# Loading the first two chunks of a weight matrix in pieces, in a LoRA and expert kernel on one core

## Chip, cores and metric

The kernel runs on one core of a Trainium2 chip. The metric is the device time of one execution in microseconds; the profile is one further execution recorded by the hardware profiler. TensorE is the matrix engine (PE in the profile, PEld its weight loads), VectorE is DVE, ScalarE is ACT, GpSimd is POOL, and SyncE (SP) only issues DMAs here. A queue named SPq or ACTq is the instruction stream of that engine where it issues DMAs.

## What is computed

All tensors are float32. x has shape (8, 512, 2048): 8 batches of 512 tokens.

```python
# conditioning layer: a dense layer and a LoRA adapter picked per batch
cond = einsum('bti,oi->bto', x, W) + b                    # W 2048 x 2048
A, Bm = lora_As[itok], lora_Bs[itok]                      # one of 32 slots, rank 16
cond = cond + 2 * einsum('btr,bro->bto', einsum('bti,bir->btr', x, A), Bm)
# top-1 routed low-rank layer, 8 experts of rank 16
logits = einsum('bsd,ed->bse', cond, route_w)
v, idx = top_k(logits, 1)
weight = one_hot(idx) * v
h  = einsum('bsd,erd->bser', cond, A_ffn)
out = x + einsum('bser,eor->bso', weight * h, Bw_ffn)
```

## The kernel before

The conditioning layer feeds only linear maps of 136 columns (8 experts x rank 16, and 8 routing columns), so the kernel never forms it. It multiplies W by the projection first. The tensor `proj` (2048 x 136) lies in `pj` as 16 blocks of 128 rows, and the kernel builds c = W^T x proj, adds each batch's adapter product, and gets a matrix m of 2048 x 136 per batch. Then each of 32 token tiles (128 tokens) takes 16 matmuls with m (`heads`, L452), a routing on VectorE (`route`) and the expert output (`delta`, L546), added to x and stored.

The change lies in the first stage. W comes in 16 chunks of 128 rows and 2048 columns, 1 MB each; chunk `oc` is loaded by `load_w(oc)` (L101) into one of four buffers. A row of a chunk is 8 KB of contiguous memory. For each chunk, `chunk_w(oc)` regroups the columns into 16 blocks `j` of 128, the order in which the tokens' transposes will need them: block j takes, from each quarter i of the row, 32 columns at 32 j. The copy (L274) writes two halves, `wv0` with j 0 to 7 and `wv1` with j 8 to 15, each in two buffers. ScalarE copies the first half and VectorE the second; for chunk 0 each half is copied by both engines, a quarter of the chunk per copy. When the copy is issued, the load of chunk `oc + 4` follows on SyncE, and for chunks 0 and 1 four more blocks of `pj` ahead of it. `fold_w(oc)` (L285) then does 16 matmuls, one for each j, with the block of `wv` as weights and `pj[:, oc, :]` as data; each float32 matmul shows as two instructions. The 16 results stay in PSUM over all chunks.

Every engine's order is written out by hand (`manual_schedule`), and each engine runs its instructions in program order. DMAs from SyncE and ScalarE also take turns on eight completion semaphores, so that a DMA is held until the transfer eight places earlier has landed.

The first loads stand on SyncE as chunk 0, chunk 1, `pj` blocks 3 to 4, chunk 2, `pj` 5 to 7, chunk 3. ScalarE issues `pj` block 0, blocks 1 to 2 and `it_i` (the adapter numbers, sent to all 128 partitions, 32 bytes each). Meanwhile TensorE runs passes over a tile of constants, `pm` (L132), whose result nobody reads:

```python
for _ in range(14):
    nc.tensor.matmul(pm, warm, warm, start=True, stop=True)
```

Between the chunks of the main loop stand other pieces of work: the adapters' row numbers (L160 to L166) and gathers (L167, L179) after chunks 4 and 7, transposes of the adapter (L316) from chunk 8 on, and the first tokens' moves.

Of the kernel before, what the change touches and what calls it, by code (L numbers as in the profile page):

```python
# [18 lines left out]
def kernel(  # L19
# [30 lines left out]
    nc = tc.nc  # L50
    P = 128
    Q = 32
    NQ = P // Q
# [6 lines left out]
    NJ = D // P  # L60
# [7 lines left out]
    HJ = NJ // 2  # L68
# [25 lines left out]
    def load_pj(c0, c1, eng=nc.sync):  # L94
        eng.dma_start(out=pj[:, c0:c1, :], in_=proj_v[:, c0:c1, :])  # L95

    w_tiles = []

    def load_w(oc):
        wt = wpool.tile([P, D], F32, tag="w", bufs=4, name=f"w_{oc}")  # L100
        nc.sync.dma_start(out=wt, in_=w[ts(oc, P), :])  # L101
        w_tiles.append(wt)

    load_pj(0, 1, nc.scalar)
    load_w(0)
    load_w(1)
    load_pj(3, 5)
    load_w(2)
    load_pj(5, 8)
    load_w(3)  # L110

    x_tiles = {}

# [14 lines left out]
    load_pj(1, 3, nc.scalar)  # L128
    nc.scalar.dma_start(out=it_i, in_=itok.to_broadcast([P, B]))
    pm = ps_s.tile([P, P], F32, tag="s", name="pm")  # L130
    for _ in range(14):
        nc.tensor.matmul(pm, warm, warm, start=True, stop=True)  # L132

    own_i = const.tile([P, B], I32, name="own_i")
# [123 lines left out]
    wv_tiles = {}  # L258

    def chunk_w(oc):  # L260
        copies = (nc.scalar.copy, nc.vector.tensor_copy)
        wv = [
            wpool.tile([P, HJ, P], F32, tag=f"wv{h}", bufs=2, name=f"wv{h}_{oc}")
            for h in range(2)
        ]
        wr = w_tiles[oc].rearrange("p (i j a) -> p j i a", i=NQ, a=Q)
        for h in range(2):
            wv_tiles[oc, h] = wv[h]
            dst = wv[h].rearrange("p j (i a) -> p j i a", a=Q)

            n = HJ // 2 if oc == 0 else HJ
            for k in range(HJ // n):
                copy = copies[1 - k] if oc == 0 else copies[h]
                copy(dst[:, ts(k, n)], wr[:, ds(h * HJ + k * n, n)])  # L274
        if oc + 4 < NO:
            if oc in (0, 1):
                load_pj(8 + 4 * oc, 12 + 4 * oc)
            load_w(oc + 4)
# [95 lines left out]
    def first_products(some, copy=nc.vector.tensor_copy):  # L374
# [4 lines left out]
        for z in some:  # L379
            m, _ = place(0, z)  # L380
            copy(m, banks[z][:, : pieces[z][2], :])

    chunk_w(0)
    for oc in range(NO):
        if oc + 1 < NO:
            chunk_w(oc + 1)
# [207 lines left out]
    for n in range(2 * NT + 4):  # L594
        t, h = divmod(n, 2)
# [36 lines left out]
        u, k = divmod(tq, TPU)  # L632
# [50 lines left out]
```

## Time and profile before

| what | value |
|---|---|
| median of 3 runs | 326.45 us (325.96 to 326.55) |
| the profiled execution | 326.17 us |
| its span in the profile | 324.4 us |
| L285, all matmuls of the folding stage | 512 instructions, 61.7 us busy, mean 280 ns |
| L132, passes over constants | 28 instructions, 6.2 us busy, mean 419 ns |
| L274, regrouping copies of half a chunk | ScalarE 1.05 us, VectorE 0.69 us |
| DMA issues of W | 16 of 1024 KB, median 11.4 us from issue to landing |

A line of the timeline gives the start and the length in microseconds, the engine, the line, the operation, what it writes and reads, how many instructions were merged, and in brackets the idle time of the engine before it with what ended it. Instructions of TensorE overlap, so their mean length is more than the distance between their starts. In the DMA windows, q1 is SyncE's queue and q10 ScalarE's; a percentage is the time of its packets as a share of the 16 DMA engines in that window. A packet is one contiguous run of memory.

### The profile page before, as it was taken

The numbers are of one execution on the slowest core, as the hardware profiler recorded it, in microseconds if no ns is written. First come the engines' busy times: TensorE is split into PE (matmuls) and PEld (weight loads), VectorE is DVE, ScalarE is ACT, GpSimd is POOL, SyncE is SP. The second block draws the span as 40 slices with busy tenths as digits, with TensorE's granted clock in tenths as the row PEclk, the third lists the DMA queues.
The fourth block names the chain that finished last, engine by engine and source line by source line (L and its number), as shares of the span: only waits on it lengthen the run. The fifth ranks groups of instructions, "written<-read, shape, count | busy, mean of one in ns | idle before, by whom it ended". The sixth has DMA issues, their size and how long they took to land.

```text
span 324.4 us, 5611 instructions
## 1 busy us (share of the span) xinstructions
PE 318.7 (98%) x2168; PEld 252.6 (78%) x2168; DVE 230.1 (71%) x408; ACT 185.4 (57%) x230; POOL 164.9 (51%) x180
## 2 busy tenths in 40 slices
PE   8999999999999999999999999999999999999994
PEld 8999999999776777777768677767676777766762
DVE  2123183468879788887887888788787887888864
ACT  3223247527958567748764976596567758770000
POOL 1002149998967676257717771946295357710000
PEclk9999999999999999999999999999999999999999
DMA  7999999953933385859395949585876759334437
GB/s 281 365 404 421 420 418 420 421 231 120 401 129 129 131 284 235 301 233 368 153 375 229 361 165 395 184 353 165 355 255 266 270 250 358 162 162 179 174 144 250
DMA packets 15306, 88.52 MB, mean 273 GB/s; under 512 B 1696, under 2 KB 4016, under 8 KB 4912
## 3 DMA queue, kind: packets, MB, share of 16 engines
q1 hardware_dynamic: 14112, 85.45, 67.2%
q0 software_dynamic: 320, 2.11, 1.6%
q10 hardware_dynamic: 848, 0.61, 0.6%
q8 instruction: 17, 0.28, 0.4%
q14 instruction: 9, 0.07, 0.1%
HBM read 54.60 MB, written 33.55 MB: 272 GB/s over the span
## 4 chain that ended last, share of the span: by engine, by line
PE 94%; DMA 4%; SPq 0%; ACT 0%; DVE 0%; issue 0%; DVEq 0%; ACTq 0%
PE ph L452 37%; PE po L546 32%; PE pc L285 16%; PE pa L361 4%; DMA w<-in_w_dram 4%; PE pg L330 1%; PE pw L508 1%; PE pe_o L546 1%; PE pbT L316 1%; PE pe_h L546 1%; ACT wv L274 0%; DVE x L559 0%; PE pq L339 0%; PE pe_s L546 0%; SPq L101 0%; SPq L95 0%
## 5 line engine op out<-in xcount | busy, mean ns | idle before, releaser
L242 POOL COPY xq<-x 32x1024 f32<-32x1024 f32 x121 | 126.7, 1047 | 77.4 <-DMA x<-in_x_dram 26.7
L242 ACT COPY xq<-x 32x1024 f32<-32x1024 f32 x135 | 140.9, 1044 | 12.0 <-DMA x<-in_x_dram 10.0
L452 PEld LDWEIGHTS ph<-m,xT 128*128 128x128 f32 x1024 | 124.7, 190 | 20.6 <-issue 16.1
L452 PE MATMUL ph<-m,xT 128*128 128x136 f32 x1024 | 129.5, 280 | 0.0
L546 PE MATMUL po<-fb,whT 128*128 128x512 f32 x240 | 111.6, 592 | 0.0
L559 DVE TENSOR_TENSOR x<-x,po 128x1024 f32<-128x1024 f32 x60 | 72.9, 1216 | 30.6 <-PE po L546 30.4
L220 DVE STREAM_TRANSPOSE xT<-xq 128x1024 f32<-128x1024 f32 x64 | 78.9, 1236 | 2.4 <-ACT xq L242 2.4
L546 PEld LDWEIGHTS po<-fb,whT 128*128 128x128 f32 x240 | 41.7, 190 | 32.0 <-issue 32.0
L285 PE MATMUL pc<-pj,wv 128*128 128x136 f32 x512 | 61.7, 280 | 0.2 <-ACT wv L274 0.2
L285 PEld LDWEIGHTS pc<-pj,wv 128*128 128x128 f32 x512 | 60.1, 190 | 1.1 <-ACT wv L274 0.4
L513 ACT COPY whT<-pw 128x128 f32<-128x128 f32 x32 | 8.5, 267 | 54.8 <-PE pw L508 54.5
L274 DVE COPY wv<-w 128x1024 f32<-128x1024 f32 (+1 forms) x17 | 12.7, 754 | 30.8 <-PE pc L285 17.8
L274 ACT COPY wv<-w 128x1024 f32<-128x1024 f32 (+1 forms) x17 | 16.9, 998 | 28.5 <-DMA w<-in_w_dram 21.8
L504 POOL TENSOR_TENSOR m<-m,c 128x408 f32<-128x408 f32 (+1 forms) x28 | 24.5, 905 | 1.3 <-ACT m L499 0.8
L499 ACT COPY m<-pa 128x408 f32<-128x408 f32 (+1 forms) x28 | 10.4, 456 | 17.6 <-PE pa L361 17.6
L167 POOL DMA_INDIRECT raw<-in_cond_b_dram,brow_i x1 | 1.4, 1434 | 24.4 <-DVE brow_i L166 24.4
L361 PE MATMUL pa<-g,ad_q 32*128 32x136 f32 x256 | 12.7, 288 | 0.0
L361 PEld LDWEIGHTS pa<-g,ad_q 32*128 32x128 f32 x256 | 10.6, 184 | 1.3
L207 POOL COPY ad_q<-raw 32x384 f32<-32x384 f32 x12 | 6.4, 536 | 9.3 <-DMA raw<-in_cond_a_dram,arow_i 8.9
L508 PEld LDWEIGHTS pw<-ident,wh 128*128 128x128 f32 x32 | 4.5, 141 | 7.4 <-issue 7.2
L463 DVE TENSOR_TENSOR ph<-ph,c0b 128x136 f32<-128x136 f32 x32 | 9.1, 284 | 1.5 <-PE ph L452 1.5
L473 DVE TENSOR_TENSOR wh<-ph,rw 128x128 f32<-128x128 f32 x32 | 9.3, 291 | 1.1
(65 smaller groups left out, 119.7 us busy)
## 6 DMA issues: line engine op xcount, KB each, us to landing
x<-in_x_dram SPq DMA_DIRECT2D x32, 1024.0 KB, 9.3
out_dram<-x SPq DMA_DIRECT2D x30, 1024.0 KB, 4.9
w<-in_w_dram SPq DMA_DIRECT2D x16, 1024.0 KB, 11.4
out_dram<-x SPq DMA_DIRECT2D x6, 256.0 KB, 2.7
fb<-in_ffn_b_dram SPq DMA_DIRECT2D x1, 1024.0 KB, 13.7
pj<-in_proj_dram SPq DMA_DIRECT2D x2, 272.0 KB, 10.8
out_dram<-x ACTq DMA_DIRECT2D x1, 256.0 KB, 2.4
pj<-in_proj_dram SPq DMA_DIRECT2D x1, 204.0 KB, 11.3
```

The lines of the kernel that those rows point to most:

```text
L220: nc.vector.transpose(dst[:, ts(h, HJ), :].rearrange("p j (g t) -> p g j t", t=Q), src.rearrange("p g (j a) -> p g j a", a=Q)[:, :, ts(h, ...
L242: copy(xq_tiles[u][ts(i, Q), :, g, :], x_tiles[u][ts(g, Q), :, ts(i, DQ)])
L274: copy(dst[:, ts(k, n)], wr[:, ds(h * HJ + k * n, n)])
L285: nc.tensor.matmul(pc[:, k, :], wv_tiles[oc, h][:, j, :], pj[:, oc, :], start=(oc == 0 and k == 0), stop=(oc == NO - 1), skip_group_check= ...
L361: nc.tensor.matmul(banks[z][:, n, :], ad_q[ts(q, Q), b // 2, 3 * part + n, :], g4[ts(q, Q), b, :], start=True, stop=True, tile_position=(q ...
L452: nc.tensor.matmul(ph_tiles[t][:, :NP], xT_tiles[t][:, j, :], m[j // JC][:, j % JC, :], start=(j == 0), stop=(j == NJ - 1),)
L463: nc.vector.tensor_tensor(ph, ph, c0b, ALU.add)
L473: nc.vector.tensor_tensor(wh.rearrange("p (e r) -> p e r", r=R), ph[:, :ER].rearrange("p (e r) -> p e r", r=R), rw.unsqueeze(2).to_broadca ...
L499: nc.scalar.copy(m, pa)
L504: nc.gpsimd.tensor_tensor(m, m, c, ALU.add)
L546: nc.tensor.matmul(part, whT_tiles[t], fb[:, ds(c, n)], start=True, stop=True)
L559: nc.vector.tensor_tensor(xs, xs, part, ALU.add)
```

## The change

Chunk 0 is loaded in four transfers of 256 KB and chunk 1 in two of 512 KB. Each transfer holds four (or eight) blocks j, which are a run of 128 (or 256) columns in each quarter of the row. VectorE does all four regrouping copies of chunk 0, each for one transfer. For chunks 1 and 2 the engines trade halves: VectorE the first, ScalarE the second; from chunk 3 on it is as before. Chunks 2 and 3 are each issued ahead of the `pj` blocks that stood in front of them. The passes over constants go from 14 to 8.

```diff
+    PIECES = {0: 4, 1: 2}
     def load_w(oc):
         wt = wpool.tile([P, D], F32, tag="w", bufs=4, name=f"w_{oc}")
-        nc.sync.dma_start(out=wt, in_=w[ts(oc, P), :])
+        n = NJ // PIECES.get(oc, 1)
+        for k in range(NJ // n):
+            dst, src = (
+                m.rearrange("p (i c) -> p i c", i=NQ)[:, :, ds(k * n * Q, n * Q)]
+                for m in (wt, w[ts(oc, P), :])
+            )
+            nc.sync.dma_start(out=dst, in_=src)
         w_tiles.append(wt)

     load_pj(0, 1, nc.scalar)
     load_w(0)
     load_w(1)
+    load_w(2)
     load_pj(3, 5)
-    load_w(2)
+    load_w(3)
     load_pj(5, 8)
-    load_w(3)
...
-    for _ in range(14):
+    for _ in range(8):
         nc.tensor.matmul(pm, warm, warm, start=True, stop=True)
...
     def chunk_w(oc):
-        copies = (nc.scalar.copy, nc.vector.tensor_copy)
+        copies = [nc.scalar.copy, nc.vector.tensor_copy]
+        if oc < 3:
+            copies.reverse()
...
-            n = HJ // 2 if oc == 0 else HJ
+            n = min(NJ // PIECES.get(oc, 2), HJ)
             for k in range(HJ // n):
-                copy = copies[1 - k] if oc == 0 else copies[h]
+                copy = copies[h] if oc else nc.vector.tensor_copy
                 copy(dst[:, ts(k, n)], wr[:, ds(h * HJ + k * n, n)])
```

## The prediction

> **What bounds the kernel now.** I read the table of busy time first, then TensorE's waits, then the start in order of time, then the DMA traffic in short windows.
>
> ```profile
> PE 318.7 (98%) x2168; PEld 252.6 (78%) x2168; DVE 230.1 (71%) x408; ACT 185.4 (57%) x230; POOL 164.9 (51%) x180
> ```
>
> TensorE is busy for 98% of the span. Its waits over the whole run are two:
>
> ```profile
> PE pm L132 <- DVE warm_a L87: 1.1, 1, 1.1
> PE pc L285 <- ACT wv L274: 0.2, 1, 0.2
> ```
>
> So from 14.87 us on, where the second wait ends, TensorE has no gap that the profile counts. Whatever moves that moment moves the end by the same amount, unless a later wait takes over. The timeline shows what stands before it:
>
> ```profile
> 1.06 6.16 PE L132 MATMUL pm<-warm 128*128 128x128 f32 x28 [1.06 <-DVE warm_a L87]
> 1.68 0.49 ACTq L129 DMA_DIRECT2D it_i<-in_itok_dram  x1
> 6.00 1.14 ACT L274 COPY wv<-w 128x512 f32<-128x512 f32 x2 [3.33 <-DMA w<-in_w_dram]
> 7.06 7.58 PE L285 MATMUL pc<-pj,wv 128*128 128x136 f32 x64
> 8.76 1.05 ACT L274 COPY wv<-w 128x1024 f32<-128x1024 f32 x1 [1.61 <-DMA w<-in_w_dram]
> 13.77 1.05 ACT L274 COPY wv<-w 128x1024 f32<-128x1024 f32 x1 [3.97 <-DMA w<-in_w_dram]
> 14.87 26.21 PE L285 MATMUL pc<-pj,wv 128*128 128x136 f32 x224 [0.23 <-ACT wv L274]
> 16.98 1.05 ACT L274 COPY wv<-w 128x1024 f32<-128x1024 f32 x1 [2.16 <-DMA w<-in_w_dram]
> 24.02 1.05 ACT L274 COPY wv<-w 128x1024 f32<-128x1024 f32 x1 [2.25 <-DMA w<-in_w_dram]
> 26.51 0.69 DVE L274 COPY wv<-w 128x1024 f32<-128x1024 f32 x1 [0.90 <-DMA w<-in_w_dram]
> ```
>
> The copies that end a wait on the DMA give the landings: chunk 0 at 6.00, chunk 1 at 8.76, chunk 2 at 13.77, chunk 3 at 16.98, chunk 5 at 24.02, chunk 6 at 26.51. TensorE folds a chunk in 3.74 us (26.21 / 7), so two chunks from 7.06 are done at 14.64; chunk 2 is ready at 13.77 + 1.05 = 14.82, and starts at 14.87. **The start of chunk 2 is the gate**, and it is a DMA gate: chunk 2 comes 5.01 us after chunk 1, where a chunk alone takes 2.49 (24.02 to 26.51). The DMA windows say why (8:9, 9:10, 14.4:16.4 and 26:28 us, in this order):
>
> ```profile
> DMA packets 463, 0.23 MB, mean 231 GB/s; under 512 B 129, under 2 KB 457, under 8 KB 457
> q1 hardware_dynamic: 234, 0.16, 62.3%
> q10 hardware_dynamic: 229, 0.07, 26.4%
> ...
> DMA packets 102, 0.28 MB, mean 276 GB/s; under 512 B 47, under 2 KB 70, under 8 KB 70
> ...
> DMA packets 546, 0.75 MB, mean 374 GB/s; under 512 B 29, under 2 KB 486, under 8 KB 486
> ...
> DMA packets 116, 0.83 MB, mean 414 GB/s; under 512 B 15, under 2 KB 15, under 8 KB 15
> ```
>
> Rows of 8 KB move at 414 GB/s. Rows of 544 B (pj) move slower, and at 9 to 10 us, while it_i's 128 rows of 32 B pass, the rate is 276 GB/s with the engines busy 79% of the time. Of the 2.52 us beyond a lone chunk, pj's 24 rows per engine (all of c3-4, half of c1-2) are 24 x 0.028 = 0.67; about 1.85 us are left for it_i.
>
> **The change, part by part.** Times are counted at chunk 2's start.
>
> 1. *Passes 14 to 8.* The 28 instructions start 0.214 us apart ((7.06 - 1.06) / 28); 16 of them end at 1.06 + 3.43 = 4.5 us. This frees TensorE 2.5 us earlier. It is worth nothing at chunk 2's start if the data isn't earlier.
>
> 2. *Chunk 0 in four pieces, chunk 1 in two.* Bytes stay; rows shrink from 8 KB to 512 B and 1 KB, since a piece takes four separate runs of each row. That is 2048 + 1024 packets for 256, or per engine 128 + 64 for 16. Price of a packet: 8 KB takes 2.49 / 8 = 0.311 us, 26.3 B/ns. In window 8:9 the two queues show 88.7% of 16 engine-us for 463 packets, six of them 8 KB: (14.2 - 1.9) / 457 = 27 ns for at most 544 B. Between landings, chunk 2 to 3 takes 3.21 - 2.49 = 0.72 us for pj's 24 rows per engine: 30 ns. The payload of 544 B at 26.3 B/ns is 20.7, so 6 to 9 ns are fixed. Packets overlap (shares over 100% elsewhere), so the lower end may be 4. With 6.5 ns: chunk 0 is 128 x (19.5 + 6.5) = 3.33 against 2.49, +0.84; chunk 1 is 64 x (38.9 + 6.5) = 2.91, +0.42. **Sum +1.25 us**; at 4 ns +0.8, at 9 ns +1.75.
>  A rule says otherwise: the Trainium skill, "DMA: Bandwidth & Descriptors", Specifications, gives 512 B as the smallest transfer at line rate. By it the sum is 0. The trace's 27 to 30 ns for 544 B is 30 to 45% over line rate, so I take the trace, and keep 0 as the far end.
>
> 3. *pj c3-4 moves behind chunk 2.* Sixteen rows per engine leave the path: 16 x 0.028 = **-0.45**. They are due at chunk 3, behind 0.58 us of slack (16.98 + 1.05 against 14.87 + 3.74), and chunk 3 now also has pj c5-7 (24 rows, 0.67) behind it instead of ahead: covered.
>
> 4. *Chunk 2's first half on VectorE.* 0.69 instead of 1.05 from landing to TensorE: **-0.36**. The second half on ScalarE is due 1.87 us later. VectorE's four copies of chunk 0 (4 x 0.425 = 1.7) and 0.69 of chunk 1 stand one after another, each under the arrival of the next piece (256 KB, 0.83 us): no cost. If pieces came together, the last would wait 1.3 us, still far ahead of its matmuls.
>
> 5. *it_i, pj c1-2 on ScalarE's queue.* Unmoved in program, but now met by SP's short rows. The two queues alternate packet by packet: in window 8:9 they moved 234 and 229. ScalarE's 32 rows per engine therefore pass beside the first 32 to 64 of SP's, not after chunk 1. it_i's 1.85 us falls upon pieces 0 to 1, and still ahead of chunk 2: the sum to chunk 2 doesn't change. 0 here, ends -1.5 (it hides in the ramp) and +0.5.
>
> 6. *SP's queue.* Six issues of some 0.4 us stand before chunk 2's instead of two loads and one pj. Some now wait for an earlier transfer's landing (eight completion semaphores in rotation): chunk 1's second half for pj c0, chunk 2 for piece 0, pj c3-4 for piece 1, chunk 3 for piece 2. Each is queued 3 us or more before its bytes are due on engines that are full: 0. Chunk 5's load waits as now for chunk 1's copies (ScalarE, some 12.8); it lands some 0.8 us early enough. POOL's queue isn't touched.
>
> Sum at chunk 2: +1.25 - 0.45 - 0.36 = **+0.44 us**, start at 15.3. Check that TensorE is ready: piece 1 is in SBUF by about 7.2, chunk 1's second half is copied by about 13.1 (chunk 2's new landing 13.77 + 1.25 - 0.45 = 14.57, less 2.49, plus 1.05), and its 16 instructions of 0.118 end at 15.0. Ready, just. Later gates all shift with chunk 2's DMA and keep 0.3 to 1 us (chunk 5 before: 24.02 + 1.05 = 25.07 for a need at 26.1). So about two microseconds of earlier TensorE are bought, and are spent waiting.
>
> The profiled execution took 326.17 us (span 324.4), the median is 326.45; 0.44 on the median gives **326.9**. About 0.2% (0.65 us) is what a measurement here tells from no change.
>
> **Rivals.**
>
> *Faster: short rows at line rate (or it_i hidden).* Then part 2 is 0 to 0.4, and the sum -0.4 to -0.8; with it_i partly in the ramp, down to -2.0, where TensorE's own work (4.5 + 2 x 3.74 = 12.0, plus its slow start) binds. For it: in 15 to 16 us the queue moved 408 GB/s with hundreds of 544 B rows. Against: 374 over two microseconds. About 325.3.
>
> *Slower: TensorE still slow when the fold begins.* The pm instructions run 421 ns, 0.214 apart; pc's run 280, 0.118 apart. The change of pace comes at 6.8 us, 5.7 us after the start, and the granted clock row shows 1.00 throughout, so the row doesn't tell it. The skill, "TensorE: Matmul & The Clock Gate", "Why this matters for your kernels", asks for 4 us of continuous work; its Part 1 says windows of 3.4 us run free of the kernel. By that, 3.4 us of passes fill a window only by luck; by the trace 5.7 were needed. Piece 0 after the passes keeps TensorE busy if it lands by 4.3; if it_i holds piece 0 to about 6.5, TensorE idles 2 us and starts slow at 7. It decides from there: each slow instruction loses 0.11 us, and 15 to 30 of them 1.6 to 3.3, of which 0.2 to 0.7 are slack. 327.5 to 329, say 328.3.
>
> *Slower: the rows aren't fed fast enough.* SP's issue of chunk 5 stood 2.1 us behind pj's 512 rows, against 0.33 elsewhere. If making 512 rows takes 2 us, the pieces come 2 us apart, and chunk 2 starts 2 us or more late: 328.5. Against: pj's rows pass at 400 per us in the trace, though queued long before.
>
> **Numbers.** Chances: gate at chunk 2 with the sum above 45% (of it 2 faster, 21 same, 22 slower: its own range is 326.1 to 327.6); faster 28% (27 faster, 1 same); slow TensorE 17% and feeding 10% (26 slower, 1 same). Together faster 0.29, same 0.23, slower 0.48. The range 325.0 to 328.5 cuts the ends of both sides.
>
> **What would show it.** Right: pc starts at 4.6 to 5, gaps before pieces and halves, chunk 2 at 15.0 to 15.6 with "DMA w" as releaser, none after. Part 2 is wrong if chunk 2 lands before 14; slow TensorE is seen in pc instructions of 421 ns; feeding in SP issues of 1 us and more and a DMA share well below 0.9 in 3 to 9 us. A wait at chunks 3 to 5, or pc running on from 4.6 without gaps, would overturn the account.

## The result, and the profile after

The changed kernel takes 327.37 us (median of 6 runs, 327.08 to 328.15), against 326.19 us for the kernel before beside it (6 runs). The ratio is 1.0038, with a 95% interval of 1.0025 to 1.0052: slower by 1.2 us. Of all runs in this document one, of late_pj below, was in a slow state (418.35 us, granted clock 0.756), and its ratio leaves that run out. The profiled execution took 327.41 us (span 325.5), 1.24 more than the one before (span 324.4).

TensorE's waits over the whole run, changed kernel:

```profile
PE pc L295 <- DVE wv L284: 1.3, 3, 0.6
PE pm L140 <- DVE warm_a L87: 1.1, 1, 1.1
PE pc L295 <- ACT wv L284: 0.5, 1, 0.5
```

Where one wait of 0.2 us stood there are now four, 1.8 us together. The timeline of the changed kernel places them:

```profile
1.06 3.78 PE L140 MATMUL pm<-warm 128*128 128x128 f32 x16 [1.06 <-DVE warm_a L87]
4.28 0.43 DVE L284 COPY wv<-w 128x512 f32<-128x512 f32 x1 [1.54 <-DMA w<-in_w_dram]
4.76 1.73 PE L295 MATMUL pc<-pj,wv 128*128 128x136 f32 x8
6.55 0.43 DVE L284 COPY wv<-w 128x512 f32<-128x512 f32 x1 [1.84 <-DMA w<-in_w_dram]
7.03 3.27 PE L295 MATMUL pc<-pj,wv 128*128 128x136 f32 x24 [0.53 <-DVE wv L284]
8.53 0.43 DVE L284 COPY wv<-w 128x512 f32<-128x512 f32 x1 [0.40 <-DMA w<-in_w_dram]
10.20 0.69 DVE L284 COPY wv<-w 128x1024 f32<-128x1024 f32 x1 [1.24 <-DMA w<-in_w_dram]
10.95 3.97 PE L295 MATMUL pc<-pj,wv 128*128 128x136 f32 x32 [0.64 <-DVE wv L284]
14.32 1.04 ACT L284 COPY wv<-w 128x1024 f32<-128x1024 f32 x1 [1.60 <-DMA w<-in_w_dram]
15.09 7.68 PE L295 MATMUL pc<-pj,wv 128*128 128x136 f32 x64 [0.17 <-DVE wv L284]
22.18 1.04 ACT L284 COPY wv<-w 128x1024 f32<-128x1024 f32 x1 [3.82 <-DMA w<-in_w_dram]
23.28 8.96 PE L295 MATMUL pc<-pj,wv 128*128 128x136 f32 x75 [0.51 <-ACT wv L284]
```

The fold begins at 4.76 instead of 7.06, and then waits for piece 1, for chunk 1's first half and for chunk 2. Chunk 2 starts at 15.09 (before: 14.87), 0.22 us late: all 2.3 us of the early start are spent. Then chunk 4 comes late as well. It starts at 23.28; before it started at 22.39. So 0.89 us stand on the path there, and TensorE's last instruction is 1.0 us later than before. No wait follows.

The DMA traffic at 4.5 to 7 us, in the kernel before and then in the changed one:

```profile
DMA packets 266, 1.03 MB, mean 412 GB/s; under 512 B 32, under 2 KB 148, under 8 KB 148
```

```profile
DMA packets 914, 0.41 MB, mean 163 GB/s; under 512 B 127, under 2 KB 914, under 8 KB 914
q1 hardware_dynamic: 814, 0.40, 72.2%
q10 hardware_dynamic: 100, 0.00, 1.9%
```

In these 2.5 us the changed kernel moves 0.4 MB instead of 1.0 MB, and its DMA engines are busy for only 74% of the time (72.2 and 1.9). it_i's 128 packets pass from 3.87 to 6.51 us; in the kernel before they passed from 8.12 to 10.79.

### The profile page after: what moved, and what is told of

Same layout as the page of the kernel before. It is cut to its first block, busy times and chain, and to the rows that moved or that the text cites. A ratio compares the mean times of both kernels' runs of the same rounds, so it can differ in the third digit from the quotient of the medians.

```text
span 325.5 us, 5589 instructions
## 1 busy us (share of the span) xinstructions
PE 318.0 (98%) x2156; PEld 251.0 (77%) x2156; DVE 231.4 (71%) x410; ACT 183.9 (56%) x228; POOL 164.8 (51%) x180
## 4 chain that ended last, share of the span: by engine, by line
PE 91%; DMA 6%; SPq 1%; ACT 0%; DVE 0%; issue 0%; DVEq 0%; ACTq 0%
PE ph L462 37%; PE po L556 32%; PE pc L295 14%; DMA w<-in_w_dram 6%; PE pa L371 4%; PE pg L340 1%; PE pw L518 1%; PE pe_o L556 1%; SPq L109 1%; PE pbT L326 1%; PE pe_h L556 1%; ACT wv L284 0%; DVE x L569 0%; PE pq L349 0%; PE pe_s L556 0%
## 5 line engine op out<-in xcount | busy, mean ns | idle before, releaser
L295 PE MATMUL pc<-pj,wv 128*128 128x136 f32 x512 | 63.4, 283 | 1.8 <-DVE wv L284 1.3
L295 PEld LDWEIGHTS pc<-pj,wv 128*128 128x128 f32 x512 | 60.9, 191 | 3.7 <-DVE wv L284 2.3
L284 DVE COPY wv<-w 128x1024 f32<-128x1024 f32 (+1 forms) x19 | 14.1, 742 | 30.9 <-PE pc L295 16.7
L284 ACT COPY wv<-w 128x1024 f32<-128x1024 f32 x15 | 15.7, 1047 | 31.2 <-DMA w<-in_w_dram 22.9
```

The lines of the kernel that those rows point to most:

```text
L295: nc.tensor.matmul(pc[:, k, :], wv_tiles[oc, h][:, j, :], pj[:, oc, :], start=(oc == 0 and k == 0), stop=(oc == NO - 1), skip_group_check= ...
```

## The experiments

Twelve kernels ran, each timed beside the kernel before. In three groups of four, that one had medians of 326.39, 326.45 and 326.40 us.

**it_i from 128 addresses (own_itok_rows), on the changed kernel.**

```diff
-    nc.scalar.dma_start(out=it_i, in_=itok.to_broadcast([P, B]))
+    nc.scalar.dma_start(out=it_i, in_=itok)
...
-        "itok": np.asarray(itok_B_0_23).reshape(1, -1),
+        "itok": np.tile(np.asarray(itok_B_0_23).reshape(1, -1), (128, 1)),
```

The second place is on the host, which lays the numbers out in memory before the kernel starts.

> The changed kernel, with the adapter numbers laid out in memory as 128 equal rows, so that each partition's 32 bytes come from an address of their own instead of all from one. Theory (the 32-byte rows of it_i hold the DMA engines up because all read one address, and short rows of W beside them suffer most): the rate at 4.5 to 7 us goes from 150 back to about 290 GB/s, chunk 0's last piece lands near 6.8 instead of 8.5, chunk 2 near 12.8 and starts near 13.5 instead of 15.09; chunk 4 lands near 20.7 and starts near 21.8 instead of 23.28; total about 325.9 against 327.4, some 1.5 us less. Rival 1 (making the descriptors of 512 rows per transfer is what limits 4.5 to 7 us): no change, 327.4 within 0.3. Rival 2 (rows of 32 bytes are slow from any address): no change either, but it_i still takes over 2 us from its first to its last packet.

Measured: 326.5 us, ratio 1.0014 (1.0005 to 1.0024). DMA traffic of this kernel at 4.5 to 7 us:

```profile
DMA packets 1370, 0.73 MB, mean 290 GB/s; under 512 B 109, under 2 KB 1370, under 8 KB 1370
```

The rate is the expected 290, and it_i's packets pass in 1.0 us (3.95 to 4.94) instead of 2.64. Only the source addresses differ, so it was the common address; both rivals fall. SyncE's issue of chunk 2 took 0.64 us here and 2.08 in the changed kernel, so the long issue went with the slow reads. Of the expected 1.5 us, 0.9 came. late_pj and own_rows_late_pj below differ in the same edit alone, and there it gained 0.7 us (326.74 to 326.04). How far the reads stretch varies: in late_pj, with the common address, they passed in 1.4 us, and the rate at 4.5 to 7 us was 228 GB/s.

The profiled execution was the slowest of its 14 runs (328.49 us), and shows something else, so its landings after 7 us are not typical. Busy time and granted clock of TensorE by windows of 2 us:

```profile
8.00:10.00 2.00, 1.34 (x12) 1.00 1.10 383
10.00:12.00 2.00, 0.41 (x3) 1.00 0.99 402
12.00:14.00 2.00, 2.00 (x15) 0.73 1.06 417
14.00:16.00 2.00, 2.00 (x11) 0.50 1.05 358
16.00:18.00 2.00, 2.00 (x18) 0.91 1.12 407
```

Columns are the window, its length, TensorE's busy time with its instructions, the granted clock, DMA share and GB/s. Chunk 1's first half came at 10.84, TensorE idled 2.24 us, and from about 12.9 us, 1.3 us after it had gone on at 11.59, the granted clock was halved for 3.4 us (0.27, 0.50 and 0.09 missing in three windows of 2 us): 11 instructions in a window that holds 20 in before_own_rows, below.

**Whole chunks, the rest of the change kept (whole_chunks).**

```diff
-    PIECES = {0: 4, 1: 2}
+    PIECES = {}
...
-    for _ in range(8):
+    for _ in range(14):
...
-            n = min(NJ // PIECES.get(oc, 2), HJ)
+            n = HJ if oc else HJ // 2
```

The last line keeps VectorE's four quarter copies of chunk 0.

> The changed kernel with chunks 0 and 1 loaded whole again and 14 passes; the order of the loads, VectorE's quarter copies of chunk 0 and the traded halves stay. Theory (short rows cost, order and traded halves gain): chunk 2 lands near 13.3 and TensorE reaches it at 14.6 without a wait, no wait at chunk 4 (landing near 20.7, ready 21.8, due 22.1); total 0.2 us below the kernel before, 326.0. Rival (the order of the pj blocks is what makes chunk 4 late): a wait of about 0.5 us at chunk 4 stays, total 326.6 or more.

Measured: 326.59 us, ratio 1.0010 (1.0002 to 1.0018), not below the kernel before. The rival's time came, but not its wait at chunk 4; both missed the mechanism. Timeline of this kernel:

```profile
11.46 6.72 PE L295 MATMUL pc<-pj,wv 128*128 128x136 f32 x56 [1.10 <-DMA pj<-in_proj_dram]
```

Chunk 1 waits 1.1 us for pj blocks 1 to 2, which stand on ScalarE's queue. At 4.5 to 7 us the two queues moved 141 and 138 packets, that is one for one. With three whole chunks first on SyncE's queue, each 544 B row of pj is paired with an 8 KB row, and the last row of pj 1 to 2 passes at 10.51; in the kernel before it passed at 8.58, since pj 3 to 4 on SyncE's queue came between. So beside whole rows the new order of loads brings a wait of its own.

**14 passes on the changed kernel (passes_14).**

```diff
-    for _ in range(8):
+    for _ in range(14):
```

> The changed kernel with 14 passes over constants again. Theory (chunks 2 and 4 are gates of the DMA): the fold begins at 7.06 instead of 4.76, chunk 1's first half is still awaited at 10.95, and nothing changes behind it: 327.4 within 0.3. Rival (the fold's slow instructions and gaps at the start cost time): 0.5 us or more below the changed kernel.

Measured: 327.39 us, ratio 1.0038 (1.0025 to 1.0052), equal to the changed kernel. The fold begins at 6.75, with one wait (0.46 us, chunk 1's first half), and chunk 2 starts at 15.34. The passes cost nothing here, and the early start brings nothing. This kernel and the one with whole chunks differ in the pieces alone: they cost 0.8 us (326.59 to 327.39).

**pj blocks 8 to 15 four chunks later (late_pj), on the changed kernel.**

```diff
-            if oc in (0, 1):
-                load_pj(8 + 4 * oc, 12 + 4 * oc)
+            if oc in (3, 4):
+                load_pj(4 * oc - 4, 4 * oc)
```

> The changed kernel with pj blocks 8 to 11 and 12 to 15 issued ahead of chunks 7 and 8 instead of chunks 4 and 5; they are used from chunk 8 on. Theory (chunk 4 waits since 56 rows of pj per DMA engine lie between chunks 3 and 4, on top of chunk 2's lateness): chunk 4 lands near 21.4 instead of 22.18, its wait of 0.5 us goes, chunk 2 is unchanged at 15.1: total 326.7, 0.7 us less. Rival (chunk 4 is late because its load is issued late, at 9.2 to 11.3 us): the wait stays, 327.4.

Measured: 326.74 us, ratio 1.0016 (1.0008 to 1.0023), where 326.7 was expected. The profiled execution was the fastest of its runs (326.19 us). TensorE's waits, then the timeline:

```profile
PE pc L295 <- DVE wv L284: 1.4, 4, 0.6
PE pm L140 <- DVE warm_a L87: 1.1, 1, 1.1
```

```profile
14.68 17.53 PE L295 MATMUL pc<-pj,wv 128*128 128x136 f32 x149 [0.17 <-DVE wv L284]
20.93 1.05 ACT L284 COPY wv<-w 128x1024 f32<-128x1024 f32 x1 [3.02 <-DMA w<-in_w_dram]
```

The wait on ScalarE's copy, chunk 4's, is gone; the others are much as they were. Chunk 4 landed at 20.93 instead of 22.18; chunk 2, which stands ahead of the moved rows, started 0.4 us earlier in this execution too, so that much of the difference isn't the edit's. The rows of pj ahead of chunk 4 made the second gate.

**The same source rows on the kernel before (before_own_rows).**

```diff
-    nc.scalar.dma_start(out=it_i, in_=itok.to_broadcast([P, B]))
+    nc.scalar.dma_start(out=it_i, in_=itok)
...
```

> The kernel before, with the adapter numbers laid out in memory as 128 rows, each read from its own address. Theory (it_i's common address holds engines up ahead of chunk 2): its packets pass in about 1 us instead of 2.65, chunk 2 lands near 12.3 instead of 13.77, chunk 2 starts at 14.64 when TensorE is ready: 0.2 us less than before, 326.2, as TensorE's own work is then the limit. Rival (with 8 KB rows beside it, it_i costs little, and chunk 2's lateness has another cause): chunk 2 lands at 13.5 or later and nothing changes.

Measured: 325.20 us, ratio 0.9965 (0.9952 to 0.9977), better than both kernels. The mechanism is the expected one and the gain larger, 1.2 us by the medians. TensorE's waits, then the timeline:

```profile
PE pm L132 <- DVE warm_a L87: 1.1, 1, 1.1
```

```profile
6.78 33.41 PE L285 MATMUL pc<-pj,wv 128*128 128x136 f32 x287
11.97 1.05 ACT L274 COPY wv<-w 128x1024 f32<-128x1024 f32 x1 [2.28 <-DMA w<-in_w_dram]
```

Chunk 2 lands at 11.97 instead of 13.77, so it_i's common address had cost 1.8 us there, and the fold runs from 6.78 without a gap. In the profiled executions the gain is 0.8 us (325.37 against 326.17): 0.3 is the earlier start, since TensorE's pace rose a little sooner in the passes, and 0.4 the missing gap at chunk 2. What the medians have beyond that wasn't traced.

**Pieces with both edits (own_rows_late_pj), and chunk 0 in two transfers (two_pieces).** The first is the changed kernel with the two edits above; the second changes one line more.

```diff
-    PIECES = {0: 4, 1: 2}
+    PIECES = {0: 2}
```

> The changed kernel with it_i from own addresses and pj blocks 8 to 15 issued four chunks later. Theory (short rows cost about 1.3 us of DMA, the common address some 1.5, and the pj rows ahead of chunks 4 and 5 make the late gate): chunk 2 starts near 13.1 to 13.5, no wait after it, total 324.6 to 325.0. Rival (short rows cost much more than 1.3 us, or a lagging engine remains): chunk 2 starts at 14.3 or later, 325.8 or more.

> As the changed kernel with it_i from own addresses and the late pj blocks, but chunk 0 in two transfers (rows of 1 KB) and chunk 1 whole (rows of 8 KB). Theory (a packet has a fixed cost of some 6 to 9 ns beyond its bytes): 64 packets per engine of 46 ns instead of 128 of 27 and 64 of 46; chunk 2 lands about 1.2 us earlier than with four and two pieces, but the fold begins some 0.5 us later, and chunk 1 is ready only as a whole: chunk 2 starts 13.0 to 13.5, total within 0.4 us of the four pieces. Rival (the fixed cost is small): 0.5 us or more slower than with four pieces.

Measured: 326.04 us, ratio 0.9992 (0.9982 to 1.0001), and 326.63 us, ratio 1.0004 (0.9994 to 1.0014). The first rival held: chunk 2 starts at 14.39, and TensorE still waits 1.1 us in all, for chunk 1's first half, chunk 2 and chunk 4. That short rows cost more than 1.3 us is shown by rows_alone below. In the second, the size is the rival's (0.6 us slower than with four pieces), but not for the rival's reason. TensorE's fold instructions at 6 to 10.5 us in the kernel with two transfers:

```profile
L295 PE MATMUL pc<-pj,wv 128*128 128x136 f32 x20 | 4.4, 408 | 1.4 <-DVE wv L284 1.4
```

They take 408 ns on average, not 280. The eight passes end at 4.5 to 4.8, piece 0 comes at 5.52, and the fold starts slow: 14 instructions of over 400 ns, to 9.6 us.

**Twelve passes on that kernel (two_pieces_12).**

```diff
-    for _ in range(8):
+    for _ in range(12):
```

> The kernel with chunk 0 in two transfers, it_i from own addresses and the late pj blocks, which began its fold at 6.27 after 1.8 us of idle TensorE and took 326.6, with 12 passes instead of 8, which end at 6.2. Nothing else differs. Theory (after the idle stretch TensorE runs slow: 14 instructions of over 400 ns, 0.11 us lost by each): the slow instructions are gone or at most two, about 1.5 us less, 325.1. Rival (the DMA holds it): 326.6 as before.

Measured: 326.08 us, ratio 0.9989 (0.9981 to 0.9997). The same window:

```profile
L295 PE MATMUL pc<-pj,wv 128*128 128x136 f32 x28 | 3.8, 286 | 1.0 <-DVE wv L284 1.0
```

No instruction of over 400 ns is left in the fold, as expected. The gain was some 0.55 us instead of 1.5, since chunk 0's second half is now awaited for 1.0 us and chunk 1 for 0.4: the slow stretch had covered part of the DMA's lateness.

**Both edits without pieces (before_own_late).** The kernel before with it_i's own rows and the late pj blocks.

> The kernel before with it_i from own addresses and pj blocks 8 to 15 issued four chunks later; chunks 0 and 1 whole, 14 passes. Theory: TensorE starts at 7.06 and nothing holds it afterwards, 326.2; against the same two edits on the changed kernel it is 1.2 to 1.6 us slower, which is what the pieces are worth when nothing else stands in the way. Rival: the same as with pieces, within 0.4 us.

Measured: 325.21 us, ratio 0.9967 (0.9955 to 0.9978). The theory's time was too high by 1 us, and its comparison had the wrong sign: the same two edits give 326.04 us on the changed kernel. The whole change (pieces, order, copies, passes) loses 0.8 us, even with the common address and the late gate out of the way.

**The short rows alone (rows_alone).** Only the transfers of chunks 0 and 1 change, on the kernel with it_i's own rows; order, copies and 14 passes as before.

```diff
-        nc.sync.dma_start(out=wt, in_=w[ts(oc, P), :])
+        n = NJ // {0: 4, 1: 2}.get(oc, 1)
+        for k in range(NJ // n):
...
+            nc.sync.dma_start(out=dst, in_=src)
```

> The kernel before with it_i from own addresses, and of the change only the transfers of chunks 0 and 1 in four and two pieces; order of the loads, copies and 14 passes as before. It prices the short rows alone: without them chunk 2 landed at 11.97 and the time was 325.2. Theory 1 (the prediction's 6.5 ns beyond the bytes, +1.25 us): chunk 2 lands near 13.2, is ready at 14.3, TensorE does not wait: 325.2. Theory 2 (the pieces cost near 2.1 us, as chunk 2's landing at 13.62 with and 11.93 without them, corrected by 0.45 us for the order, suggests): chunk 2 lands near 14.1, starts near 15.2 instead of 14.2: 326.0 to 326.5.

Measured: 327.13 us, ratio 1.0028 (1.0018 to 1.0037); without the pieces it was 325.20. Timeline of this kernel:

```profile
7.37 0.62 ACT L280 COPY wv<-w 128x512 f32<-128x512 f32 x1 [1.05 <-DMA w<-in_w_dram]
11.54 0.69 DVE L280 COPY wv<-w 128x1024 f32<-128x1024 f32 x1 [4.53 <-DMA w<-in_w_dram]
14.57 1.05 ACT L280 COPY wv<-w 128x1024 f32<-128x1024 f32 x1 [3.49 <-DMA w<-in_w_dram]
15.67 24.60 PE L291 MATMUL pc<-pj,wv 128*128 128x136 f32 x208 [0.57 <-ACT wv L280]
```

Chunk 2 lands at 14.57 instead of 11.97. **The short rows cost 2.6 us at chunk 2's landing, not 1.25**, and more than theory 2's 2.1; in the time they cost 1.9 us. own_itok_rows is this kernel with the rest of the change (order, copies, 8 passes) and took 326.50, so that rest gains 0.6 us beside short rows. The rates by window (same columns as above), this kernel and then the one with whole chunks:

```profile
4.00:6.00 2.00, 2.00 (x11) 1.00 1.12 307
6.00:8.00 2.00, 2.00 (x19) 1.00 1.04 287
8.00:10.00 2.00, 2.00 (x20) 1.00 1.05 346
```

```profile
4.00:6.00 2.00, 2.00 (x11) 1.00 1.01 406
6.00:8.00 2.00, 2.00 (x18) 1.00 0.97 397
8.00:10.00 2.00, 2.00 (x19) 1.00 1.12 414
```

At 307 GB/s chunk 0 takes 3.4 us and at 346 chunk 1 takes 3.0, against 2.49 each: 1.5 us. About 1.1 us remain. The windows show the mean over 16 engines, and some rows lag behind it: chunk 1's last 1 KB row ends at 10.97, when 8 KB rows of chunk 2, which stand behind it on the same queue, have been passing since 9.61. In the kernel with whole chunks the rows that follow chunk 1 (pj 3 to 4) begin at 7.88 and chunk 1's last row ends at 8.2, an overlap of 0.3 us instead of 1.4. A lag of this size would account for the rest; that it does wasn't tested. In that trace a 1 KB packet took 1161 ns at 7.7 us; the changed kernel had 512 B packets of 1821 and 1473 ns at 4.8. That kernel with whole chunks had none over 620 ns in 4 to 12 us; the kernel before, with the common address, had three of 691 to 742 ns. Why single packets stick is open.

**Twelve passes with whole chunks (before_own_12), and 14 with pieces (own_late_14).**

```diff
-    for _ in range(14):
+    for _ in range(12):
```

The first edits the kernel before_own_rows; the second edits own_rows_late_pj, from 8 to 14.

> The kernel before with it_i from own addresses and 12 passes instead of 14. Theory (with chunk 2 in time, only the start of the fold limits, and chunk 0's first quarter is copied at 6.35, before the 14 passes end at 6.8): the fold begins at 6.4, no wait at chunks 1 to 5, 324.8, some 0.4 us less than with 14 passes. Rival (the passes end before the clock is released, and the first instructions of the fold run slow): no gain or up to 0.5 us slower, 325.2 to 325.7.

> The changed kernel (four and two pieces) with it_i from own addresses, the late pj blocks and 14 passes instead of 8. With 8 it took 326.0, its runs between 325.4 and 327.0. Theory (gaps at the start make TensorE's pace vary, and chunk 2 near 14.4 is the gate): the runs lie closer together, median 325.3 to 325.6. Rival (what it loses against the whole chunks is the DMA's alone): 326.0 as with 8.

Measured: 325.11 us, ratio 0.9963 (0.9950 to 0.9976), and 326.31 us, ratio 0.9999 (0.9988 to 1.0009). In the first, the fold begins at 6.38 and no wait follows, as the theory said, and no run of slow instructions stands at its start. But the median is only 0.1 us below that with 14 passes, where 0.4 was expected; the runs can't tell it from nothing. In the second the theory fell: its runs lie from 325.55 to 327.36, no closer than with 8 passes, and TensorE waits once, for chunk 1's first half:

```profile
PE pc L295 <- DVE wv L284: 0.9, 1, 0.9
```

No instruction at the start of the fold ran slow in this trace, which speaks against TensorE's pace as the source of the spread. That half landed at 10.35, and at 9.51 with 8 passes, so the landing of the pieces differs between executions.

## Why the prediction was right, point by point

The forecast of 326.9 us leaned to slower, and slower it was, by 1.2 us for the 0.44 of the sum. The main view held in part: chunk 2 is a DMA gate, and a start 2.3 us earlier is spent in waiting before it. It was forecast to start at 15.3, and started at 15.09. That this came so near was luck: with the short rows at their measured cost the sum would have put it at 16.65, and about 1.6 us came off elsewhere. And a wait at one of chunks 3 to 5, which the prediction had named as a sign against its account, did come, at chunk 4.

1. *Passes.* Right: the last of them ends by 4.8 (forecast 4.5), and 14 give the same time (passes_14).
2. *Short rows, +1.25 us.* The mechanism was right and the term mis-sized: 2.6 us (rows_alone). The trace of before had short rows only mixed with 8 KB rows; almost alone they ran at 287 to 346 GB/s, and single packets stuck. The sign named for this part, chunk 2 before 14, stayed away and still said nothing about the size, since another term was wrong the other way. The skill's line rate from 512 B ("DMA: Bandwidth & Descriptors", Specifications) does not hold here, by these rates.
3. *pj 3 to 4 behind chunk 2, -0.45.* Not tried alone. That its rows are covered at chunk 3 was right, as there is no wait there.
4. *First half on VectorE, -0.36.* Right: from landing to start 0.77 us (14.32 to 15.09), before 1.10.
5. *it_i, 0.* **Wrong.** Its common address cost 1.8 us at chunk 2 in the kernel before (13.77 to 11.97). In the changed kernel chunk 2 lands at 14.32 with it, and at 13.62 and 14.44 in the two kernels with own rows and the late pj (at 14.94 in the profiled execution of own_itok_rows). By these single traces the change hid 1.1 us or more, towards the far end of -1.5. The medians, in which other gates have a share, say less: the own rows gained 1.2 us on the kernel before and 0.9 and 0.7 on the changed one, so some 0.4 to 0.6 were hidden. How much it was, and so what else the sum at chunk 2 lacked, stays open.
6. *SyncE's queue, 0.* Its issues took longer than assumed: the pieces 0.61 to 0.66 us each, chunk 2's 2.1. No gate was traced to them.
7. *"Later gates keep 0.3 to 1 us".* **This failed.** With pj 5 to 7 moved behind chunk 3, 56 rows per engine lie between chunks 3 and 4 instead of 32, and chunk 4 came 0.5 us too late for a fold already 0.2 late. late_pj removes that wait, and 0.6 us.

What made the kernel slower is the pieces: without them the rest of the change is within 0.2 us of the kernel before (whole_chunks), and with them it takes 0.8 us more (passes_14).

The rival of a slow TensorE was no fancy, but it did not decide. The changed kernel has three slow instructions at the start (5.15 to 5.6 us); the kernel with two transfers had 14, and 12 passes took them away. The slow stretch in own_itok_rows lasted 3.4 us (12.93 to 16.34), the length of the skill's free-running windows ("TensorE: Matmul & The Clock Gate", Part 1). That part gives about one idle window before the clock falls; in this one execution 2.24 us of idling were enough. If the window before the fall ran from 9.52 to 12.93, it held 2.1 us of idling and 1.3 us of work; that such a window counts as idle is an inference from this trace alone.

The rival of slow feeding had its sign in the changed kernel, an issue of 2.1 us and a DMA share of 0.72 at 4 to 6 us. But with it_i's own rows the same short pieces ran at 290 GB/s in the window in which they had run at 163, and the issue took 0.64 us. So the common address had made the sign.

## What to carry to other kernels

An early start is worth only what the next late arrival leaves of it: follow each gate downstream with its own arrivals, and count how many rows lie between two chunks after a reordering. Splitting a load into column pieces shortens its rows; here whole 8 KB rows in the old order with the start at 6.6 us (before_own_late) were 0.8 us better than the changed kernel's pieces with the start at 4.9 (own_rows_late_pj). Price such rows where they run alone, as a mixed window had shown half of their cost. A tiny broadcast load is worth a look: 4 KB read from one address cost the kernel before 1.2 us, and giving each partition its own row made both kernels faster.

## What the runs showed of the hardware

- 128 reads of one 32-byte address took 2.64 to 2.67 us from first to last packet in the two kernels first compared (1.4 us in late_pj). At 4.5 to 7 us in the changed kernel, most of that time, the DMA engines moved 163 GB/s at a busy share of 0.74. From 128 addresses they took 1.0 us, at 290 GB/s and a share above 1 (own_itok_rows).
- Two queues with work moved packets one for one: 234 and 229 in 1 us (kernel before, 8 to 9 us), and 141 and 138 in 2.5 us, where one had rows of 8 KB and the other of 544 B (whole_chunks). So a short row beside long ones came at the long rows' pace; it_i's own rows beside rows of 1 and 8 KB took 2.1 and 3.4 us (two_pieces_12, two_pieces), with the engines busy (share 1.05).
- In rows_alone, 512 B rows moved at 307 GB/s (4 to 6 us) and 1 KB rows at 314 (7.2 to 8.8 us); 8 KB rows moved at 397 to 414 in before_own_rows. In the changed kernel 1 KB rows reached 375 (8 to 9.6 us).
- After 2.24 us of idling the granted clock fell to half for 3.4 us in one execution, beginning 1.3 us after work had resumed (own_itok_rows).
